# Cross attention of a Perceiver block: the norm and bias of the keys applied at the scores, the last key tiles of two batches shared, and the ternary weights' sums on another engine

## Chip, cores and metric

One NeuronCore of a Trainium2 chip runs the whole program. The metric is the device time of one execution in microseconds (us); lower is better. The program is written in Bass with the Tile layer, whose scheduler puts the instructions of each engine in a fixed order when the program is built. Engines are called TensorE (PE), VectorE (DVE), ScalarE (ACT), GpSimd (POOL) and SyncE (SP, which here issues every DMA).

## What is computed

A Perceiver block: 8 batches of 64 tokens with 512 features (`x`) attend to themselves and to a context of 1601 rows per batch (`ctx`); a small sparse attention and a ternary two-layer network follow. The change is in the attention to the context and in the preparation of the network's weights:

```
kx, vx = split(einsum(cond, w_kv_x))          # cond: 8 x 1601 x 512
kx = LN(kx) * kxln_w + kxln_b                 # over each head's 128 features, 8 key heads
p  = softmax(qx . kx / sqrt(128))             # 2 query heads for each key head
xout = p . vx
...
scale = mean(abs(w)); w = sign(w) * (abs(w) >= 0.7 * scale)    # both ffn weights
```

All matrix products are held to float32 accuracy: an operand is split into a high part in a rounded format (float32r) and the rest, and three products (high-high, high-rest, rest-high) are added in PSUM.

## The kernel before

**Units and tiles.** The context attention is cut into 16 units, one for each half of the key heads (4 heads, `HG`) and each batch: `Cross(b, half)`. The half is the outer loop. A unit's 1601 keys are 13 tiles: twelve of 128 keys and a last one of 65. The tiles form six chunks (`CHUNKS`, line 36): five of two tiles (256 keys), and a last one of three (128 + 128 + 65 = 321 keys).

**One key tile.** `keys` (line 529) loads 128 columns of the transposed context (`cTr`), ScalarE makes the high part (`cThi`, 536), GpSimd the rest (`cTlo`, 537), and TensorE runs twelve matmuls with 512 moving columns (542), the context standing in the array and the key weights moving. The weights have had each head's mean taken off (`key_weights`), so the product needs no mean. ScalarE squares it (547) and copies it to `kn` (548); VectorE sums the squares per head (549); GpSimd adds epsilon (550) and raises to the power -1/2 (`rsqrt`, line 173, tile `rqk`); VectorE multiplies `kn` by that (552). `keys_t` (555) transposes `kn` on TensorE (219), and makes the two parts of the keys, with the norm's weight and bias: `kthi` on ScalarE (565), the rest on VectorE (`kf`, 567), and again ScalarE for the bias (`ktlo`, 568).

**Scores.** `scores` (570) multiplies the queries with a chunk's keys (587) into a PSUM bank of the pool `pm` (three banks, tag `m`, shared with the transposes of the probabilities `pt` and others); each bank holds two heads' scores, or one's in the last chunk. A custom VectorE operation (591) copies the scores to SBUF, adding zeros, and keeps the row's maximum. `maxima` (594) forms the maximum of a unit, `exps` (598) the exponentials on ScalarE (601). `probs_t` (604) transposes the probabilities and splits them (`phi`, `plo`, 623 and 624), `context` (636) loads the context rows again (`cr`) and splits them (`chi`, `clo`), and `weigh` (661) sums probability times context over the 13 tiles (676 to 678, accumulators `acc`).

**Order.** The main loop (line 1142) runs one key tile per step: keys of tile g, their transposition one step later, scores of a chunk two steps after its last key tile, probabilities and context 16 to 17 steps behind (`LAG`). Into each step generators put other work at a given pace: projections and self-attention (`bgA`), the last parts (`bgC`), and `ternary` (918, `bgB`), which reads both network weights in 32 pieces, sums their absolute values on VectorE (926), and then reads them again to make the ternary weights. The scheduler then orders all engines' instructions; SP's list of DMAs is one queue, and a DMA that waits for an engine holds up those behind it.

Of the kernel before, what the change touches and what calls it, by code (L numbers as in the profile page):

```python
# [11 lines left out]
F32 = mybir.dt.float32  # L12
# [9 lines left out]
P = 128  # L22
H = 512
NIC = 4
# [12 lines left out]
KTW = 324  # L37
NCH = len(CHUNKS)
CHUNK_OF = {tt: ci for ci, ch in enumerate(CHUNKS) for tt in ch}
LAG = 17  # L40
# [6 lines left out]
LATER = 142  # L47
TERNARY_PACE, TERNARY_AT = 0.4, 8
HELD = "held"

# [7 lines left out]
def tile_perceiver(ctx: ExitStack, tc: tile.TileContext, t: dict):  # L58
# [18 lines left out]
    def nm(s):  # L77
        uid[0] += 1
        return f"{s}_{uid[0]}"
# [62 lines left out]
    class Late:  # L142
# [11 lines left out]
        xrt = _main("qxhi", 1)  # L154
        pd = _main("kf", 2)
        ps = staticmethod(lambda tag="b": kxp())
# [334 lines left out]
    def key_weights(half):  # L491
        hi = mp.tile([P, NIC, 512], F32R, tag="wkhi", name=nm("wkhi"), bufs=1)
        lo = mp.tile([P, NIC, 512], F32R, tag="wklo", name=nm("wklo"), bufs=1)
        for ic in range(NIC):
            tag, bufs = ("kf", 2) if half == 0 and ic >= 2 else ("raw", 3)
            raw = load(mp.tile([P, 512], F32, tag=tag, name=nm("wkr"), bufs=bufs), t["wkv"][ic * P:(ic + 1) * P, half * 512:(half + 1) * 512])
            raw3 = v3(raw, HG)
            mu = sm("wkmu", HG)
            V.tensor_reduce(mu, raw3, AX.X, ALU.add)
            V.scalar_tensor_tensor(raw3, mu.unsqueeze(2).to_broadcast([P, HG, D]), -1.0 / D, raw3, ALU.mult, ALU.add)  # L500
            A.copy(hi[:, ic, :], raw)
            (V if half else GP).tensor_tensor(lo[:, ic, :], raw, hi[:, ic, :].bitcast(F32), ALU.subtract)
        return hi, lo

    paced = [None]
    pin = [None]

    class Cross:


        def __init__(self, b, half):
            self.b, self.half = b, half
            self.raw = None
            self.S = {}
            self.kt = {}
            self.kn = {}
            self.pp = {}
            self.cc = {}
            self.mx = sm("cmx", HG * NCH, bufs=2)
            self.su = sm("csu", HG * NCH, bufs=2)  # L520

# [7 lines left out]
        def keys(self, tt):  # L529

            t0, n = TT[tt]
            raw = mp.tile([P, NIC, P], F32, tag="raw", name=nm("cTr"), bufs=3)
            paced[0] = nc.sync.dma_start(raw[:, :, :n], t["ctxT"][self.b].rearrange("(c p) k -> p c k", p=P)[:, :, t0:t0 + n])
            chi = mp.tile([P, NIC, P], F32R, tag="cThi", name=nm("cThi"), bufs=2)
            clo = mp.tile([P, NIC, P], F32R, tag="cTlo", name=nm("cTlo"), bufs=2)
            A.copy(chi[:, :, :n], raw[:, :, :n])  # L536
            GP.tensor_tensor(clo[:, :, :n], raw[:, :, :n], chi[:, :, :n].bitcast(F32), ALU.subtract)  # L537
            ps = kxp()
            k = 0
            for st, mv in ((chi, self.wk[0]), (chi, self.wk[1]), (clo, self.wk[0])):  # L540
                for ic in range(NIC):
                    PE.matmul(ps[:n], lhsT=st[:, ic, :n], rhs=mv[:, ic, :], start=k == 0, stop=k == 11)  # L542
                    k += 1
            kn = mp.tile([P, 512], F32, tag="kn", name=nm("kn"), bufs=3)
            sq = mp.tile([P, 512], F32, tag="sq", name=nm("sq"), bufs=1)
            v = sm("kxv", HG)
            A.activation(sq[:n], ps[:n], AF.Square, scale=1.0 / math.sqrt(D))  # L547
            A.copy(kn[:n], ps[:n])
            V.tensor_reduce(v[:n], v3(sq[:n], HG), AX.X, ALU.add)  # L549
            GP.tensor_scalar(v[:n], v[:n], EPS, None, ALU.add)  # L550
            r = rsqrt(v[:n], n, HG, "rqk")
            pin[0] = V.tensor_tensor(v3(kn[:n], HG), v3(kn[:n], HG), r.unsqueeze(2).to_broadcast([n, HG, D]), ALU.mult)  # L552
            self.kn[tt] = kn

        def keys_t(self, tt):

            t0, n = TT[tt]
            ci = CHUNK_OF[tt]
            c0 = TT[CHUNKS[ci][0]][0]
            if ci not in self.kt:  # L560
                self.kt[ci] = [mp.tile([P, HG, KTW], F32R, tag="kt" + x, name=nm("kt" + x), bufs=2) for x in ("hi", "lo")]
            hi, lo = self.kt[ci]
            pt = transpose4(self.kn.pop(tt), n, kxp())
            o = slice(t0 - c0, t0 - c0 + n)
            A.activation(hi[:, :, o], v3(pt, HG)[:, :, :n], AF.Identity, bias=hb["kx"], scale=hw["kx"])  # L565
            kf = mp.tile([P, HG, P], F32, tag="kf", name=nm("kf"), bufs=2)
            V.scalar_tensor_tensor(kf[:, :, :n], v3(pt, HG)[:, :, :n], hw["kx"], hi[:, :, o].bitcast(F32), ALU.mult, ALU.subtract)  # L567
            A.activation(lo[:, :, o], kf[:, :, :n], AF.Identity, bias=hb["kx"])  # L568

        def scores(self, ci):  # L570
# [3 lines left out]
            N = cw + (cw & 1)  # L574
            if N > cw:
                GP.memset(hi[:, :, cw:N].bitcast(F32), 0.0)
                GP.memset(lo[:, :, cw:N].bitcast(F32), 0.0)
            sc = mp.tile([P, HG, KTW], F32, tag="S", name=nm("S"), bufs=7)
            self.S[ci] = sc
            per = 512 // N  # L580
            for g0 in range(0, HG, per):
# [7 lines left out]
                for i, g in enumerate(gs):  # L589
                    ps = bank[:, i * N:(i + 1) * N]  # L590
                    V.tensor_tensor_reduce(sc[:, g, :cw], ps[:, :cw], zeros.to_broadcast([P, cw]), 1.0, -3.0e38,  # L591
                                           ALU.add, ALU.max, self.mx[:, g * NCH + ci:g * NCH + ci + 1])

        def maxima(self):
            self.nmx = sm("cnm", HG)
            V.tensor_reduce(self.nmx, v3(self.mx, HG), AX.X, ALU.max, negate=True)  # L596

# [320 lines left out]
    def ternary(name, dst):  # L918
# [4 lines left out]
        for k in range(nr * ncb):  # L923
            r, cb = k // ncb, k % ncb
            raw = load(tern(), w[r * P:(r + 1) * P, cb * 512:(cb + 1) * 512])
            V.tensor_reduce(su[:, k:k + 1], raw, AX.X, ALU.add, apply_absolute_value=True)
            yield
# [17 lines left out]
    def ffn_rows(pairs, kind):  # L945
# [22 lines left out]
        return z, xs  # L968

    def gp_copy(dst, src):  # L970
        GP.tensor_scalar(dst, src, 1.0, 1.0, ALU.mult, ALU.mult)  # L971

# [156 lines left out]

    NT = len(TT)  # L1130
    work = [Cross(b, half) for half in range(2) for b in range(NB)]
# [10 lines left out]
    for g in range(NA + LAG + 3):  # L1142
# [25 lines left out]
        if g < NA:  # L1168
            work[nA].keys(kA)
        if g == 0:  # L1170
            bgA.pump(ALL)
        if g == 2:
            bgA.add(norms(rest), projection("qx", range(4), rest), projection("qx", range(4, 8), range(NJ)),
                    projection("q", range(8), range(NJ)), projection("k", range(4), range(NJ)), projection("v", range(4), range(NJ)))
            bgA.add(*[self_attn(j) for j in range(NJ)])
            bgA.add(attn_consts())
# [132 lines left out]
```

## Time and profile before

| | us |
|---|---|
| runs: median (lowest to highest of 3) | 2002.96 (2000.17 to 2003.44) |
| the profiled execution: its time / its span | 1998.47 / 1996.7 |
| TensorE idle, 0 to 100 us | 24.2 |
| TensorE idle, 100 to 1800 us | 25.0 |
| TensorE idle, 1800 to 1997 us | 16.3 |

The span is from the first to the last instruction that the profiler recorded; the execution's time is 1.8 us more. "Busy" for TensorE is the union of its matmuls' records, which overlap, so small gaps between them are not seen in it.

A row of a group gives line, engine, operation, the tiles written and read, the shape, how many, then the busy time and the mean duration of one, and the idle time of the engine before them with what ended it. Two of them:

```
L568 ACT ACTIVATE ktlo<-kf,cols 128x512 fp32r<-128x512 f32 (+1 forms) x208 | 147.4, 709 | 29.0 <-DVE kf L567 28.5
L552 DVE TENSOR_TENSOR kn<-kn,rqk 128x512 f32<-128x512 f32 (+1 forms) x208 | 144.7, 695 | 57.0 <-POOL rqk L173 55.5
```

A row of a timeline gives start and length in us, engine, line, operation, tiles, the size of the array used, the shape and the number of instructions merged.

### The profile page before, as it was taken

What the parts mean: (1) busy time and instruction counts of PE and PEld (TensorE: products, weight loads), DVE (VectorE), ACT (ScalarE), POOL (GpSimd) and SP (SyncE); (2) the same over time, 40 slices, a digit from 0 to 9 for tenths busy, and PEclk for the clock granted to TensorE, in tenths of its full rate; (3) what the DMA queues carried; (4) which work ended last, traced back from release to release, by engine and by line L of the source; (5) the groups of instructions that cost most, each with busy time, mean ns of one, the idle gap of its engine ahead of it and who ended that gap; (6) DMA issues with size and microseconds to landing.
All of it is one profiled execution on the core that took longest, in us unless ns stands there. A gap on an engine that the chain in (4) does not pass through costs nothing. (4 is left out here: it accounts for less than half of the span.)

```text
span 1996.7 us, 32526 instructions
## 1 busy us (share of the span) xinstructions
PE 1931.5 (97%) x10709; PEld 1594.1 (80%) x10709; DVE 1357.9 (68%) x3324; ACT 1345.9 (67%) x2932; POOL 682.7 (34%) x807
## 2 busy tenths in 40 slices
PE   6899999999999999999999999999999999999998
PEld 5688887888888888888888888888877777886776
DVE  6868678667778677766775765666577665665665
ACT  6777777677778667765765655665786676676554
POOL 5443434333334434323233323323333323320132
PEclk9999999999999999999999999999999999999989
DMA  6354445466455654556886667656744633564415
GB/s 195 112 151 148 148 146 153 132 193 213 152 150 172 194 179 140 173 180 224 282 268 192 214 225 264 203 185 214 258 133 154 212 110 97 165 205 139 149 56 172
DMA packets 296507, 352.05 MB, mean 176 GB/s; under 512 B 30337, under 2 KB 191233, under 8 KB 296337
## 3 DMA queue, kind: packets, MB, share of 16 engines
q1 hardware_dynamic: 296336, 349.97, 55.8%
q8 instruction: 84, 1.38, 0.3%
q14 instruction: 87, 0.70, 0.1%
HBM read 283.94 MB, written 65.68 MB: 175 GB/s over the span
## 5 line engine op out<-in xcount | busy, mean ns | idle before, releaser
L537 POOL TENSOR_TENSOR cTlo<-cTr,cThi 128x512 fp32r<-128x512 f32 (+1 forms) x208 | 271.1, 1303 | 840.7 <-PE kx L542 443.8
L677 PE MATMUL acc<-plo,chi 128*128 128x512 f32 x768 | 311.7, 406 | 1.0 <-DVE plo L624 1.0
L678 PE MATMUL acc<-phi,clo 128*128 128x512 f32 x768 | 303.4, 396 | 0.0
L549 DVE TENSOR_REDUCE kxv<-sq 128x4 f32<-128x512 f32 (+1 forms) x208 | 141.9, 682 | 228.0 <-ACT sq L547 227.7
L542 PE MATMUL kx<-wkhi,cThi 128*128 128x512 f32 (+1 forms) x832 | 244.3, 415 | 6.6 <-DVE cmx L591 2.5
L676 PE MATMUL acc<-phi,chi 128*128 128x512 f32 x768 | 237.8, 403 | 4.6 <-ACT chi L653 3.4
L565 ACT ACTIVATE kthi<-kx,cols 128x512 fp32r<-128x512 f32 (+1 forms) x208 | 159.5, 767 | 106.8 <-PE kx L219 105.1
L542 PE MATMUL kx<-wklo,cThi 128*128 128x512 f32 (+1 forms) x832 | 231.0, 398 | 0.0
L542 PE MATMUL kx<-wkhi,cTlo 128*128 128x512 f32 (+1 forms) x832 | 226.3, 393 | 0.0
L173 POOL TENSOR_TENSOR rqk<-kxv,mhalf 128x4 f32<-128x4 f32 (+1 forms) x208 | 219.9, 1057 | 16.6
L653 ACT CAST chi<-cr 128x512 fp32r<-128x512 f32 x192 | 118.9, 619 | 137.7 <-PE acc L677 126.2
L536 ACT CAST cThi<-cTr 128x512 fp32r<-128x512 f32 (+1 forms) x208 | 125.6, 605 | 120.0 <-PE kx L542 48.4
L601 ACT ACTIVATE S<-S,cnm 128x256 f32<-128x256 f32 (+1 forms) x384 | 196.8, 520 | 1.5 <-DVE cnm L596 1.5
L567 DVE SCALAR_TENSOR_TENSOR kf<-kx,cols,kthi 128x512 f32<-128x512 f32 (+1 forms) x208 | 151.1, 726 | 60.0 <-ACT kthi L565 58.8
L542 PEld LDWEIGHTS kx<-wklo,cThi 128*128 128x128 f32 (+1 forms) x832 | 156.2, 188 | 39.7
L542 PEld LDWEIGHTS kx<-wkhi,cTlo 128*128 128x128 f32 (+1 forms) x832 | 153.5, 185 | 39.3 <-issue 0.8
L552 DVE TENSOR_TENSOR kn<-kn,rqk 128x512 f32<-128x512 f32 (+1 forms) x208 | 144.7, 695 | 57.0 <-POOL rqk L173 55.5
L542 PEld LDWEIGHTS kx<-wkhi,cThi 128*128 128x128 f32 (+1 forms) x832 | 147.2, 189 | 40.8 <-DVE cmx L591 5.0
L591 DVE CUSTOM_DVE_ANT_0 S<-s,zeros 128x256 f32<-128x256 f32 (+1 forms) x384 | 149.7, 429 | 43.8 <-PE s L587 43.5
L568 ACT ACTIVATE ktlo<-kf,cols 128x512 fp32r<-128x512 f32 (+1 forms) x208 | 147.4, 709 | 29.0 <-DVE kf L567 28.5
L676 PEld LDWEIGHTS acc<-phi,chi 128*128 128x128 f32 x768 | 139.0, 189 | 34.9 <-ACT chi L653 4.6
L677 PEld LDWEIGHTS acc<-plo,chi 128*128 128x128 f32 x768 | 145.2, 189 | 25.7 <-DVE plo L624 1.5
(339 smaller groups left out, 3938.3 us busy)
## 6 DMA issues: line engine op xcount, KB each, us to landing
cTr<-in_ctxT SPq DMA_DIRECT2D x192, 256.0 KB
cr<-in_ctx SPq DMA_DIRECT2D x192, 256.0 KB
ws<-wpd SPq DMA_DIRECT2D x88, 512.0 KB
clod<-clo SPq DMA_DIRECT2D x96, 256.0 KB
clo<-clod SPq DMA_DIRECT2D x96, 256.0 KB
wv<-in_wkv SPq DMA_DIRECT2D x64, 256.0 KB
tern<-in_ffn_w SPq DMA_DIRECT2D x64, 256.0 KB
wpd<-ws SPq DMA_DIRECT2D x32, 512.0 KB
```

The source lines that it names most:

```text
L173: GP.tensor_tensor(y[:n], v, mhalf[:n, :k], ALU.pow)
L537: GP.tensor_tensor(clo[:, :, :n], raw[:, :, :n], chi[:, :, :n].bitcast(F32), ALU.subtract)
L542: PE.matmul(ps[:n], lhsT=st[:, ic, :n], rhs=mv[:, ic, :], start=k == 0, stop=k == 11)
L552: pin[0] = V.tensor_tensor(v3(kn[:n], HG), v3(kn[:n], HG), r.unsqueeze(2).to_broadcast([n, HG, D]), ALU.mult)
L565: A.activation(hi[:, :, o], v3(pt, HG)[:, :, :n], AF.Identity, bias=hb["kx"], scale=hw["kx"])
L567: V.scalar_tensor_tensor(kf[:, :, :n], v3(pt, HG)[:, :, :n], hw["kx"], hi[:, :, o].bitcast(F32), ALU.mult, ALU.subtract)
L568: A.activation(lo[:, :, o], kf[:, :, :n], AF.Identity, bias=hb["kx"])
L591: V.tensor_tensor_reduce(sc[:, g, :cw], ps[:, :cw], zeros.to_broadcast([P, cw]), 1.0, -3.0e38, ALU.add, ALU.max, self.mx[:, g * NCH + ci:g ...
L601: A.activation(self.S[ci][:, g, :cw], self.S[ci][:, g, :cw], AF.Exp, bias=self.nmx[:, g:g + 1], accum_out=self.su[:, g * NCH + ci:g * NCH ...
L676: PE.matmul(self.U[ic], lhsT=chi[:n, s], rhs=phi[:n], start=tt == 0, stop=False)
L677: PE.matmul(self.U[ic], lhsT=chi[:n, s], rhs=plo[:n], start=False, stop=False)
L678: PE.matmul(self.U[ic], lhsT=clo[:n, s], rhs=phi[:n], start=False, stop=False)
```

## The change

1. **Norm at the scores.** A key's factor r (one per key and head) is no longer multiplied into `kn`. The raw keys are transposed; `turned` makes both parts with the norm's weight alone. r is stored to DRAM tile by tile (`rd`), and when a chunk's last tile is stored, `spread` loads the chunk's values into all 128 partitions (`rb`, keys by heads, 324 x 4 floats, two buffers). The VectorE operation of the scores multiplies by `rb[:, :cw, g]` in place of adding zeros.
2. **Bias at the scores.** The norm's bias adds the same number to all of a row's scores, which a softmax does not see. It stands as one more column behind the last chunk's 321 keys (the place of a zero column before), its score is copied to `qb`, and `maxima` forms the maximum as qb - (max + qb).
3. **Paired last tiles.** From batch 2 of half 0 on, the last tile's first 64 keys of two batches share one tile of 128: the even batch computes it (tile `kn2`, factors `rt`), the odd one has no thirteenth key tile. The remaining key 1600 of all eight batches is computed once for each half by `odd_keys`, at steps 30 and 110; its transposed parts are copied behind the 64 keys.
4. **Absolute sums on ScalarE.** `ternary` forms them with an activation (absolute value, with a running sum) in place of VectorE's reduction.
5. The buffers `kf` give way to `rb`; the program is built with `dynamic_dma_scratch_size=1024`.

The core of the diff:

```diff
+NT = len(TT)
+ODD_AT = 30, 110
+UNPAIRED = 2
+RB = 2
...
+    def raw_keys(wk, chi, clo, n, held=False):
+
+        ps = kxp()
+        k = 0
+        for st, mv in ((chi, wk[0]), (chi, wk[1]), (clo, wk[0])):
+            for ic in range(NIC):
+                PE.matmul(ps[:n], lhsT=st[:, ic, :n], rhs=mv[:, ic, :], start=k == 0, stop=k == 11)
+                k += 1
+        kn = mp.tile([P, 512], F32, tag="kn2" if held else "kn", name=nm("kn"), bufs=1 if held else 3)
+        sq = mp.tile([P, 512], F32, tag="sq", name=nm("sq"), bufs=1)
+        v = sm("kxv", HG)
+        A.activation(sq[:n], ps[:n], AF.Square, scale=1.0 / math.sqrt(D))
+        A.copy(kn[:n], ps[:n])
+        pin[0] = V.tensor_reduce(v[:n], v3(sq[:n], HG), AX.X, ALU.add)
+        GP.tensor_scalar(v[:n], v[:n], EPS, None, ALU.add)
+        r = rsqrt(v[:n], n, HG, "rqk")
+        return kn, r
+
+    def turned(kn, n, parts, r0=0):
+
+        hi, lo = parts
+        pt = kxp()
+        for g in range(HG):
+            PE.transpose(pt[:, g * P:g * P + n], kn[:, g * P:(g + 1) * P], ident[r0:r0 + n, r0:r0 + n])
+        src = v3(pt, HG)[:, :, :n]
+        A.activation(hi, src, AF.Copy, scale=hw["kx"])
+        V.scalar_tensor_tensor(lo, src, hw["kx"], hi.bitcast(F32), ALU.mult, ALU.subtract)
+
+    def odd_keys(half):
+
+        raw = load(mp.tile([P, 512], F32, tag="raw", name=nm("oc"), bufs=3)[:NB], t["ctx"][:, SC - 1, :])
+        pt = kxp()
+        for ic in range(NIC):
+            PE.transpose(pt[:, ic * NB:(ic + 1) * NB], raw[:, ic * P:(ic + 1) * P], ident[:NB, :NB])
...
+        kn, r = raw_keys(wk[half], chi, clo, NB)
+        oddr[half] = dtile([NB, HG], F32, f"oddr{half}")
+        nc.sync.dma_start(oddr[half], r)
...
+        turned(kn[:NB], NB, [x[:, :, :, 0] for x in oddk[half]])
...
         def keys(self, tt):
...
+            pair = tt == NT - 1 and self.paired
+            if pair and self.b % 2:
+                return
...
-            pin[0] = V.tensor_tensor(v3(kn[:n], HG), v3(kn[:n], HG), r.unsqueeze(2).to_broadcast([n, HG, D]), ALU.mult)
+            kn, r = raw_keys(self.wk, chi, clo, n, pair)
             self.kn[tt] = kn
+            if pair:
+                nxt = work[self.half * NB + self.b + 1]
+                nxt.kn[tt] = kn
+                self.rt = nxt.rt = dram.tile([P, HG], F32, tag="rt", name=nm("rt"), bufs=2)
+                nc.sync.dma_start(self.rt, r)
+                return
...
+            nc.sync.dma_start(self.rd[ci][o:o + n], r)
+
+        def spread(self, ci):
+            cw = sum(TT[tt][1] for tt in CHUNKS[ci])
+            rb = self.rb[ci] = mp.tile([P, KTW, HG], F32, tag="rb", name=nm("rb"), bufs=RB)
+            parts = [(0, self.rd.pop(ci)[:cw])]
+            if ci == NCH - 1 and self.paired:
+                o = cw - S - 1
+                parts = [(0, parts[0][1][:o]), (o, self.rt[self.b % 2 * S:(self.b % 2 + 1) * S]), (cw - 1, oddr[self.half][self.b:self.b + 1])]
+            for o, src in parts:
+                w = src.shape[0]
+                load(rb[:, o:o + w].rearrange("p t g -> p (t g)"), src.rearrange("t g -> (t g)").partition_broadcast(P))
...
-            A.activation(hi[:, :, o], v3(pt, HG)[:, :, :n], AF.Identity, bias=hb["kx"], scale=hw["kx"])
-            kf = mp.tile([P, HG, P], F32, tag="kf", name=nm("kf"), bufs=2)
-            V.scalar_tensor_tensor(kf[:, :, :n], v3(pt, HG)[:, :, :n], hw["kx"], hi[:, :, o].bitcast(F32), ALU.mult, ALU.subtract)
-            A.activation(lo[:, :, o], kf[:, :, :n], AF.Identity, bias=hb["kx"])
...
-                    V.tensor_tensor_reduce(sc[:, g, :cw], ps[:, :cw], zeros.to_broadcast([P, cw]), 1.0, -3.0e38,
-                                           ALU.add, ALU.max, self.mx[:, g * NCH + ci:g * NCH + ci + 1])
+                    V.tensor_tensor_reduce(sc[:, g, :cw], ps[:, :cw], rb[:, :cw, g], 1.0, -3.0e38,
+                                           ALU.mult, ALU.max, self.mx[:, g * NCH + ci:g * NCH + ci + 1])
+                    if N > cw:
+                        V.tensor_copy(self.qb[:, g:g + 1], ps[:, cw:N])
 
         def maxima(self):
+
+            top = sm("ctop", HG)
+            V.tensor_reduce(top, v3(self.mx, HG), AX.X, ALU.max)
+            V.tensor_tensor(top, top, self.qb, ALU.add)
             self.nmx = sm("cnm", HG)
-            V.tensor_reduce(self.nmx, v3(self.mx, HG), AX.X, ALU.max, negate=True)
+            V.tensor_tensor(self.nmx, self.qb, top, ALU.subtract)
...
-            V.tensor_reduce(su[:, k:k + 1], raw, AX.X, ALU.add, apply_absolute_value=True)
+            A.activation(raw, raw, AF.Abs, accum_out=su[:, k:k + 1])
...
         if g < NA:
             work[nA].keys(kA)
+            if kA == CHUNKS[CHUNK_OF[kA]][-1]:
+                work[nA].spread(CHUNK_OF[kA])
...
+        if g in ODD_AT:
+            odd_keys(work[nA].half)
```

## The prediction

> **What bounds the kernel now.** I read the engines' shares of the page first, then the same by stretch.
>
> ```profile
> PE 1931.5 (97%) x10709; PEld 1594.1 (80%) x10709; DVE 1357.9 (68%) x3324; ACT 1345.9 (67%) x2932; POOL 682.7 (34%) x807
> ...
> q1 hardware_dynamic: 296336, 349.97, 55.8%
> ```
> ```profile
> 0.00:100.00 100.00, 75.82 (x382) 61.57 (x383) 76.31 (x215) 71.43 (x149) 51.82 (x67) 0.94 0.51 154
> 100.00:1800.00 1700.00, 1674.99 (x9332) 1398.89 (x9332) 1161.25 (x2827) 1167.78 (x2580) 587.08 (x692) 0.99 0.58 183
> 1800.00:1997.00 197.00, 180.73 (x998) 133.59 (x994) 120.37 (x283) 106.64 (x206) 43.78 (x49) 0.94 0.43 130
> ```
>
> The columns of the second are length, then busy time of PE, PEld, DVE, ACT and POOL, then clock, DMA share and GB/s. In the 1700 us of key work TensorE lacks only 25 us; VectorE and ScalarE stand at 68%. So a microsecond counts only if it is taken from TensorE's list, or from a wait of TensorE. The chain that ended last covers only the last 25 us, the two-layer network at the end, which the change does not touch. A matmul's record overlaps the next one's, so its 390 ns is not its price. The price is from one start to the next; the timeline of one last key tile gives it:
>
> ```profile
> 1109.59 1.17 PE L542 MATMUL kx<-wkhi,cThi 128*65 128x512 f32 x4
> 1110.59 1.09 PE L542 MATMUL kx<-wklo,cThi 128*65 128x512 f32 x4
> 1111.52 1.09 PE L542 MATMUL kx<-wkhi,cTlo 128*65 128x512 f32 x4
> 1112.55 1.16 PE L485 MATMUL po<-fb,ld 64*128 64x128 f32 x8
> ```
>
> Twelve matmuls from 1109.59 to 1112.55: 2.96 us for 65 keys. A full tile next to it (1118.71, 1119.72, 1120.64) steps at the same 0.92 to 1.01 us per four. The 512 moving columns set the price, not the keys.
>
> **Pairing of the last tiles.** In the built order of the changed kernel 201 key tiles stand where 208 did, seven fewer (three in half 0, four in half 1), and two tiles of eight keys come in (odd_keys). Removed: 7 x 2.96 = 20.7 us (by steps of 0.92: 19.3). Added: 2 x 2.96 = 5.9 us (5.5), and 16 transposes of 8 rows, by the 128-wide rows of 0.35 to 0.44 us per four 0.1 us each, 1.6 us. All this lies on TensorE: -13.2 us (-12.2 to -13.5). TensorE's other matmuls are the same in number and shape. The odd unit's missing tile also spares ScalarE and GpSimd five tiles net, 9 and 13 us there, hidden. The kept tile kn2 has one buffer, but its next writer comes 25 tiles later: no wait.
>
> **Norm moved to the scores, off the path.** Rows by line (busy us, mean ns), then TensorE's waits:
>
> ```profile
> L591 DVE CUSTOM_DVE_ANT_0 S<-s,zeros 128x256 f32<-128x256 f32 x320 | 119.7, 418 | 28.5 <-PE s L587 28.3
> ...
> L897 DVE TENSOR_REDUCE ao<-pr 128x64 f32<-128x384 f32 x3 | 2.5, 832 | 0.0
> ...
> L926 DVE TENSOR_REDUCE tsumffn_w<-tern 128x1 f32<-128x512 f32 x32 | 21.7, 679 | 0.0
> ```
> ```profile
> PE pt L613 <- DVE cmx L591: 3.9, 5, 1.4
> ...
> PE kx L219 <- DVE kn L552: 3.0, 2, 1.9
> ...
> PE kx L542 <- DVE cmx L591: 2.5, 6, 0.6
> ```
>
> VectorE loses the 208 products of L552 (144.7 us) and the 32 sums of L926 (21.7). It gains 64 copies of one column from PSUM (164 ns by the copy of L817: 10 us) and two 128x4 operations for each of 16 maxima (169 ns by L596: 5 us). ScalarE loses the 208 passes of L568 (147.4 us) and gains 32 absolute sums: 630 ns as L803, plus 197 ns for the accumulator as in L601, 26 us. No table load is added in the built order.
>
> The score operation now reads rb with a step of four floats. The row: a step of two floats (L885) costs nothing, 357 ns for 192 elements; a step of 64 floats (L897) costs 832 ns for 384, where a plain product of 384 (L882) takes 552, so 0.73 ns more for each. No row has a step of four. The Trainium skill ("SBUF — State Buffer", under "Door 1: The DMA port swizzle") says that SBUF is read in lines of 16 bytes and that a stream which takes one element from each line pays; four floats is exactly there. By the row of L885 the operation stays at 418 ns and the sum on VectorE is -151 us. By the rule with L897's size it takes 418 + 256 x 0.73 = 605 ns, 384 of them add 75 us, and the sum is -76 us. I take the rule. Either way VectorE ends below 68%. What this can touch is the PSUM bank: a bank holds two groups, so it is freed 0.4 us later. TensorE waited for such a bank eleven times (6.4 us); eleven times 0.4 is 4 us, the lower queue of VectorE gives some back, so +2 us (0 to +8).
>
> What goes from TensorE's waits: L219 no longer waits for the product, -3.0 us (both waits fall in the first 60 us); and with VectorE relieved by 76 us and ScalarE by some 125, part of the other 20 us of TensorE's waits on them, -2 us (0 to -8). If the new maxima chain were bare, 16 x 1 us would be lost; but TensorE waited only 2.8 us for the exponentials that hang on it, so I count it in the +2.
>
> **The new wait: r goes through DRAM.** Each tile's rqk is written out (207 small stores and 2 of eight rows), and a load of 512 KB spreads a chunk over the partitions (96, of which 14 have two small loads beside them), all on SP: 329 more DMAs than the 1368 in the built order. The score operation waits for it, and on VectorE everything stands behind that: the key sums L549, plo L624, the splits. Time needed, from the store and load of sim:
>
> ```profile
> 1488.23 2.30 SPq L830 DMA_DIRECT2D simd<-fa  x4
> 1491.78 0.50 SPq L130 DMA_DIRECT2D sim<-simd  x1
> ```
>
> The last of the four stores starts at 1490.03, and the load that waits for it goes out at 1491.78: 1.75 us (2.7 in another pass, at 1808). GpSimd reads sim at 1493.86, 2.1 us on. The spread moves 0.52 MB; at 350 MB in 55.8% of 1997 us the engines move 314 GB/s when busy, so 1.7 us more. Issue, store and load: 0.5 + 1.75 to 2.7 + 3.8 = 6 to 7 us. Time there is:
>
> ```profile
> 1115.90 1.09 POOL L173 TENSOR_TENSOR rqk<-kxv,mhalf 65x4 f32<-65x4 f32 x1
> ```
> ```profile
> 1129.32 0.49 DVE L591 CUSTOM_DVE_ANT_0 S<-s,zeros 128x321 f32<-128x321 f32 x1
> ```
>
> Here 12.3 us; over the 96 chunks the median is 16.0, the tenth lowest 12.3, the least 8.4. In the changed order, at the old steps, 17 us of matmuls (old: 16.3) lie between a chunk's last key matmul and its first score matmul, of which rqk takes 3.4; the first chunks have 9 to 12 us. So mid-kernel the load has 6 us in hand and costs nothing; in the first 100 us four chunks come 0.5 us late or so: +2 us (0 to +8). If that cover went, 96 chunks would pay.
>
> SP's queue: a store waits for GpSimd's rqk, and a spread for the store's landing, up to 2 us in the 33 chunks where they stand next to each other. Behind them stand the loads of keys (cTr) and of context (cr) and the stores of clo. SP waited up to 7.6 us in one place already. But cThi was ready 13.3 us (median) before the matmul that reads it, and chi 11.4 us, so a few microseconds there are covered: 0. DMA share: 52 MB more, 8 points by bytes and up to 5 by packets: 64 to 69%, hidden. The smaller scratch for dynamic DMA touches no queue that the profile shows: 0.
>
> **Sum.** -13.2 - 3.0 - 2 + 2 + 2 = -14.2 us. The profiled execution took 1998.47 us (span 1996.7 and 1.8 around it), so 1984.3. The median of the runs, 2002.96, lies 4.5 us higher: 1989 us.
>
> **Rivals.** *The spread comes late* (slower). Place: the score operation's wait for rb. If the way through DRAM and SP's queue takes 14 to 15 us instead of 6 to 7, more than the 13 us between rqk and the score matmuls, VectorE stands some 2 us in each of 96 chunks; TensorE has plo in hand by 3.45 us (median), 1.04 (tenth lowest), so about 0.5 us of each reaches it: +48 - 13 = +35, 2038 us. For it: SP's waits of 5 to 7 us, pieces of 16 bytes, one queue for all. Against: the 6 us in hand. It decides from about 13 us on. Chance 0.2. *Given back in small waits*: banks held longer (+8), start (+8), nothing gained on other waits: about 1999 to 2006, within 0.2% of before, which is about what a measurement of this kernel can tell from no change. Chance 0.08. *The relief counts for more*: TensorE's waits of the middle shrink by 8 to 10 us: 1979 us. Chance 0.08. That the change does not remove the matmuls is excluded by the built order.
>
> **Numbers.** The likeliest, 1989 us (own range 1982 to 1997), has 0.64. Faster by over 0.2%: 0.64 + 0.08 = 0.72; same 0.08; slower 0.20. The range from 1977 to 2012 takes in all but the far part of the late spread (0.14) and a little below.
>
> **What would show it.** Right: 201 full key tiles; TensorE's busy time down by about 13 us and still 97%; no wait of VectorE for rb past the first 100 us; the score row near 605 ns (418 would refute the rule here); VectorE near 1280, ScalarE near 1220 us; DMA share 64 to 69%. Wrong: a row in which S waits for rb with some 100 us, TensorE waiting for plo or for a bank, cThi waiting for cTr; or TensorE's share falling to 95%.

## The result, and the profile after

| | before | after |
|---|---|---|
| median of 4 runs each, us | 2003.16 | 2095.69 (2089.53 to 2101.72) |
| ratio, 95% interval | | 1.0465 (1.0432 to 1.0498) |
| profiled execution: time / span, us | 1998.47 / 1996.7 | 2089.53 / 2087.8 |
| clock granted to TensorE, mean share of the full one | 0.987 | 0.977 |

The change makes the kernel 92.5 us slower, where 1989 us had been forecast. From the profile's page of after, its engines and the hardware DMA queue:

```profile
PE 1959.4 (94%) x10665; PEld 1600.2 (77%) x10665; DVE 1297.7 (62%) x3182; ACT 1223.5 (59%) x2803; POOL 679.1 (33%) x766
...
q1 hardware_dynamic: 343068, 402.86, 64.3%
```

VectorE and ScalarE lost what had been forecast (1280 and 1220 us forecast, 1298 and 1224 found), and the DMA share lies at the lower end of the forecast 64 to 69%. But TensorE is busy 28 us longer instead of 13 us shorter, and its share has fallen to 94%. The stretches of after (length, then busy time of PE, PEld, DVE, ACT and POOL, clock, DMA share, GB/s):

```profile
0.00:100.00 100.00, 69.58 (x333) 57.40 (x334) 64.03 (x179) 55.26 (x119) 47.72 (x63) 0.88 0.56 165
100.00:1800.00 1700.00, 1621.55 (x8848) 1335.49 (x8847) 1059.27 (x2593) 1009.37 (x2358) 566.40 (x629) 0.98 0.67 202
1800.00:2088.00 288.00, 268.29 (x1487) 207.34 (x1486) 174.44 (x411) 158.84 (x327) 64.97 (x75) 0.97 0.52 159
```

In the 1700 us of key work TensorE now lacks 78 us where it lacked 25, and ends them 484 matmul records behind. The matmuls themselves are not slower where nothing disturbs them. One tile in the timeline of after:

```profile
1171.59 1.17 PE L527 MATMUL kx<-wkhi,cThi 128*128 128x512 f32 x4
1172.60 1.10 PE L527 MATMUL kx<-wklo,cThi 128*128 128x512 f32 x4
1173.54 1.08 PE L527 MATMUL kx<-wkhi,cTlo 128*128 128x512 f32 x4
1174.54 0.46 PE L544 MATMUL kx<-ident,kn 64*128 64x64 f32 x4
1178.07 1.22 PE L435 MATMUL pp<-ws,cats 128*128 128x512 f32 x2 [3.06 <-DMA ws<-wpd]
1179.09 1.48 PE L771 MATMUL acc<-phi,chi 128*128 128x512 f32 x3
```

Twelve matmuls from 1171.59 to 1174.54 take 2.95 us, as before. Then TensorE stands 3.06 us for a load of weights, and after the pause two matmuls take 1.02 us from start to start, twice their pace. The groups by shape, the score operation and the split of the loaded keys:

```profile
L680 DVE CUSTOM_DVE_ANT_0 S<-s,rb 128x256 f32<-128x256 f32 x320 | 179.3, 605 | 26.3 <-PE s L676 25.2 <-DMA cr<-in_ctx 0.8
L680 DVE CUSTOM_DVE_ANT_0 S<-s,rb 128x321 f32<-128x321 f32 x64 | 46.1, 721 | 15.3 <-PE s L676 10.7 <-DMA rb<-rd 2.7 <-DMA rb<-rt 1.8
L611 ACT CAST cThi<-cTr 128x512 fp32r<-128x512 f32 x199 | 123.7, 621 | 266.8 <-DMA cTr<-in_ctxT 168.7 <-PE kx L527 45.5 <-issue 34.4
```

The score operation takes 605 ns, the forecast number, and waits for `rb` 4.5 us in all (2.7 + 1.8). So r itself comes in time but for these; it is the other loads that are late. ScalarE waits 168.7 us for `cTr`. In the waits of before the same line was

```profile
ACT cThi L536 <- DMA cTr<-in_ctxT: 16.0, 16, 3.0
```

(us in all, times, longest) and in the waits of after, of ScalarE and TensorE:

```profile
ACT cThi L611 <- DMA cTr<-in_ctxT: 168.7, 64, 6.9
...
PE pp L435 <- DMA ws<-wpd: 16.4, 12, 3.1
...
PE s L676 <- DVE cmx L680: 8.1, 4, 3.7
PE pt L708 <- DVE cqb L683: 6.5, 5, 1.9
...
PE pt L708 <- DVE cmx L680: 3.9, 5, 1.8
```

What SP's queue waits for in after:

```profile
SPq L134 <- DMA rd<-rqk: 147.2, 78, 4.8
SPq L626 <- POOL rqk L177: 146.7, 127, 9.0
```

78 spreads stand 1.9 us each for a store to land, 127 stores 1.2 us each for GpSimd. One place in the timeline, SP and ScalarE:

```profile
1167.01 0.38 SPq L626 DMA_DIRECT2D rd<-rqk  x1
1167.48 0.38 SPq L134 DMA_DIRECT2D clo<-clod  x1
1170.12 0.32 SPq L134 DMA_DIRECT2D rb<-rd  x1
1170.49 0.43 SPq L608 DMA_DIRECT2D cTr<-in_ctxT  x1
1171.02 0.92 SPq L134 DMA_DIRECT2D ws<-wpd  x2
...
1176.85 0.62 ACT L611 CAST cThi<-cTr 128x512 fp32r<-128x512 f32 x1 [4.22 <-DMA cTr<-in_ctxT]
```

The spread goes out 3.1 us after the store; `cTr` and `ws` go out right behind it. ScalarE stands 4.22 us for `cTr`, and TensorE its 3.06 us for `ws` (above). This picture suggested the first theory: SP's in-order queue, held by the two new waits, delays the loads behind them. It is the theory that the experiments had to test.

### The profile page after: what moved, and what is told of

Its sections match the earlier page's. It is cut to its first block, busy times and chain, and to the rows that moved or that the text cites. A ratio compares the mean times of both kernels' runs of the same rounds, so it can differ in the third digit from the quotient of the medians.

```text
span 2087.8 us, 32963 instructions
## 1 busy us (share of the span) xinstructions
PE 1959.4 (94%) x10665; PEld 1600.2 (77%) x10665; DVE 1297.7 (62%) x3182; ACT 1223.5 (59%) x2803; POOL 679.1 (33%) x766
## 4 chain that ended last, share of the span: by engine, by line
PE 61%; DMA 20%; DVE 7%; ACT 5%; issue 3%; POOL 2%; SPq 1%; POOLq 0%; ACTq 0%; DVEq 0%
PE kx L527 19%; PE acc L771 6%; DMA cTr<-in_ctxT 6%; PE acc L772 6%; PE acc L773 5%; PE s L676 4%; PE pj L344 3%; PE pt L708 3%; PE kx L544 3%; DMA ws<-wpd 2%; PE xo L792 2%; DMA wpd<-ws 2%; PE pp L435 2%; DVE S L680 2%; PE p L900 1%
## 5 line engine op out<-in xcount | busy, mean ns | idle before, releaser
L612 POOL TENSOR_TENSOR cTlo<-cTr,cThi 128x512 fp32r<-128x512 f32 (+1 forms) x201 | 260.9, 1298 | 784.5 <-ACT cThi L611 396.8
L611 ACT CAST cThi<-cTr 128x512 fp32r<-128x512 f32 (+1 forms) x201 | 124.5, 619 | 268.3 <-DMA cTr<-in_ctxT 168.7
L680 DVE CUSTOM_DVE_ANT_0 S<-s,rb 128x256 f32<-128x256 f32 (+1 forms) x384 | 225.4, 625 | 41.6 <-PE s L676 36.0
L527 PE MATMUL kx<-wkhi,cThi 128*128 128x512 f32 x812 | 238.9, 415 | 12.5 <-ACT kn L533 3.3
L527 PE MATMUL kx<-wklo,cThi 128*128 128x512 f32 x812 | 230.8, 405 | 0.0
L527 PE MATMUL kx<-wkhi,cTlo 128*128 128x512 f32 x812 | 227.7, 399 | 0.0
L547 DVE SCALAR_TENSOR_TENSOR ktlo<-kx,cols,kthi 128x512 fp32r<-128x512 f32 (+2 forms) x208 | 150.7, 725 | 99.8 <-ACT kthi L546 98.6
L546 ACT ACTIVATE kthi<-kx,cols 128x512 fp32r<-128x512 f32 (+2 forms) x208 | 140.5, 676 | 79.8 <-PE kx L544 79.0
L527 PEld LDWEIGHTS kx<-wklo,cThi 128*128 128x128 f32 x812 | 155.8, 192 | 39.6 <-issue 1.6
L527 PEld LDWEIGHTS kx<-wkhi,cTlo 128*128 128x128 f32 x812 | 153.7, 190 | 39.8 <-issue 2.4
L527 PEld LDWEIGHTS kx<-wkhi,cThi 128*128 128x128 f32 x812 | 146.3, 192 | 48.4 <-DVE cmx L680 5.4
L773 PEld LDWEIGHTS acc<-phi,clo 128*128 128x128 f32 x768 | 145.5, 190 | 25.3 <-issue 0.8
```

Source lines behind the costliest of these rows:

```text
L546: A.activation(hi, src, AF.Copy, scale=hw["kx"])
L547: V.scalar_tensor_tensor(lo, src, hw["kx"], hi.bitcast(F32), ALU.mult, ALU.subtract)
L680: V.tensor_tensor_reduce(sc[:, g, :cw], ps[:, :cw], rb[:, :cw, g], 1.0, -3.0e38, ALU.mult, ALU.max, self.mx[:, g * NCH + ci:g * NCH + ci + 1])
L773: PE.matmul(self.U[ic], lhsT=clo[:n, s], rhs=phi[:n], start=False, stop=False)
```

## The experiments

"Over before" is the median of the run less that of before among the same job's runs (before lay between 1997.9 and 2000.8 us in the five jobs).

| run | us | over before | ratio, 95% interval |
|---|---|---|---|
| e1_norm_back | 2015.28 | +15.4 | 1.0089 (1.0062 to 1.0115) |
| e2_spread_only | 2041.63 | +41.8 | 1.0219 (1.0184 to 1.0255) |
| e3_trip_only | 2065.72 | +65.8 | 1.0336 (1.0306 to 1.0366) |
| e4_const_rb | 2023.37 | +23.5 | 1.0121 (1.0094 to 1.0147) |
| e5_sums_on_vector | 2017.92 | +17.2 | 1.0089 (1.0068 to 1.0111) |
| e6_no_bias_column | 2011.02 | +10.3 | 1.0060 (1.0039 to 1.0081) |
| e7_unpaired | 2015.35 | +14.6 | 1.0076 (1.0048 to 1.0104) |
| e8_before_abs | 2013.30 | +12.6 | 1.0064 (1.0043 to 1.0086) |
| e9_order_ternary | 2015.69 | +17.8 | 1.0082 (1.0061 to 1.0102) |
| e10_order_pace | 2000.27 | +2.3 | 1.0007 (0.9997 to 1.0018) |
| e11_gpsimd_queue | 2078.33 | +80.4 | 1.0388 (1.0358 to 1.0419) |
| e12_const_rb_step1 | 2008.89 | +11.0 | 1.0049 (1.0033 to 1.0065) |
| e13_stale_spread | 2086.18 | +85.5 | 1.0414 (1.0377 to 1.0451) |
| e14_stale_all | 2059.59 | +59.0 | 1.0294 (1.0271 to 1.0318) |
| e15_stores_only | 2051.14 | +50.5 | 1.0259 (1.0231 to 1.0287) |
| e16_pair_only | 2003.80 | +3.2 | 1.0009 (0.9995 to 1.0022) |
| e17_gp_stores | 2124.93 | +124.2 | 1.0609 (1.0568 to 1.0650) |
| e18_old_stores | 2080.37 | +79.6 | 1.0374 (1.0333 to 1.0415) |

### Which part of the change costs

**e1_norm_back** takes the norm back to VectorE, and with it all stores and spreads away:

```diff
+        pin[0] = V.tensor_tensor(v3(kn[:n], HG), v3(kn[:n], HG), r.unsqueeze(2).to_broadcast([n, HG, D]), ALU.mult)
...
-            nc.sync.dma_start(self.rd[ci][o:o + n], r)
...
-                    V.tensor_tensor_reduce(sc[:, g, :cw], ps[:, :cw], rb[:, :cw, g], 1.0, -3.0e38,
+                    V.tensor_tensor_reduce(sc[:, g, :cw], ps[:, :cw], zeros.to_broadcast([P, cw]), 1.0, -3.0e38,
```

> The changed kernel with the norm's factor multiplied into kn on VectorE again (no stores of r, no spread, scores copied with zeros); the bias column, the paired last tiles and the absolute sums on ScalarE stay. If the way of r through DRAM or the slower score operation costs the 93 us, this runs at 1985 to 1995 us, some 10 to 15 under the kernel before. If the pairing, the bias column, the sums on ScalarE or the new order of the program cost them, it stays above 2060 us.

**e2_spread_only** keeps the spreads, but reads them from rows of an input that is always there, and stores nothing:

```diff
-                self.rd[ci] = dram.tile([KTW, HG], F32, tag="rd", name=nm("rd"), bufs=3)
-            o = t0 - TT[CHUNKS[ci][0]][0]
-            nc.sync.dma_start(self.rd[ci][o:o + n], r)
+                self.rd[ci] = t["wkv"][self.b, :KTW * HG].rearrange("(t g) -> t g", g=HG)
```

> The changed kernel with the spread of each chunk loaded from rows of an input, and no stores of r: the same 52 MB of spread traffic, but nothing on SP waits for r or for a store's landing. The scores are scaled by other numbers than r. Theory of SP's queue (loads stand behind the store-and-spread trip): about 2010 us. Theory of traffic (the spreads hold the DMA engines and make the key loads land late): 2080 us or more, cThi still waiting for cTr with over 100 us. If both share it: near 2050.

**e3_trip_only** keeps the stores, and in place of the spread of 512 KB loads 2 KB of what was stored; the scores take a constant tile:

```diff
-                load(rb[:, o:o + w].rearrange("p t g -> p (t g)"), src.rearrange("t g -> (t g)").partition_broadcast(P))
+                load(rb[:min(w, P)], src[:min(w, P)])
...
-            rb = self.rb.pop(ci)
+            rb = rbc
```

> The changed kernel with the stores of r kept and each spread replaced by a load of the same stored values of 2 KB, on the same place in SP's queue and with the same wait for the store's landing; the score operation reads a constant tile of rb's layout. The scores are scaled by a constant in place of r. Theory of SP's queue: 2080 us. Theory of traffic: 2010 to 2020 us, cThi's wait for cTr back below 40 us.

**e4_const_rb** has the constant tile and neither stores nor loads of r.

> The changed kernel with neither stores nor spreads; the score operation reads a constant tile of rb's layout (step of four floats, 605 ns). The scores are scaled by a constant in place of r. If the trip or the traffic is the cause: 1990 to 2000 us. If the slower score operation, which frees its PSUM bank later, is the cause: 2060 us or more. TensorE's waits for banks freed by the score operation stay near 25 us in either case if they come from its length, and fall below 10 if they come from late keys.

e1, e3 and e4 fell between the two times that their texts give, e2 near the one for a shared cause. Counted from e4 (+23.5), the spread's traffic alone adds 18.3 us (e2), stores with a small load 42.3 (e3), and the two together, as in the changed kernel, 69.0 (92.5 - 23.5). So most of the loss belongs to the way through DRAM. For the stores this is not the new order alone: compared place by place in the traces, e15 below (stores and no load, 27.0 us over e4) has another instruction than e4 at 216 of ScalarE's 2803 places and e3 at 439, but e2 at 1110, so that the 18.3 of the spreads could be order (e9, below, measures a change of order alone). What is left without it, 15.4 us in e1, was still not the forecast gain of 13 us.

**e12_const_rb_step1** asks what the step of four floats costs. It is e4 with the same order of instructions; only the layout of the constant tile differs:

```diff
-    rbc = ctile([P, KTW, HG], F32, "rbc")
+    rbc = ctile([P, HG, KTW], F32, "rbc")
...
-                    V.tensor_tensor_reduce(sc[:, g, :cw], ps[:, :cw], rb[:, :cw, g], 1.0, -3.0e38,
+                    V.tensor_tensor_reduce(sc[:, g, :cw], ps[:, :cw], rb[:, g, :cw], 1.0, -3.0e38,
```

> As e4_const_rb (no stores, no spread, a constant tile in place of rb; the scores are multiplied by 0.05 instead of r), but the constant tile is laid out so that the score operation reads it with a step of one float instead of four; the order of the instructions is that of e4. If the 8 us between e4 and e1 are the score operation's length (605 against 418 ns): 418 ns again and about 2015. If they are the order: 2023 as e4, though the operation is short. A row that stays near 605 ns would say that not the step but the second SBUF operand costs.

The line's durations (ns, least/median/most, both shapes together), first in e4, then in e12:

```profile
L661 DVE CUSTOM_DVE_ANT_0 S<-s,rbc x384: 547/606/758, 51.8 to 1820.6; 128x256 f32<-128x256 f32 x160, 128x321 f32<-128x321 f32 x32
```
```profile
L661 DVE CUSTOM_DVE_ANT_0 S<-s,rbc x384: 372/420/495, 53.7 to 1806.2; 128x256 f32<-128x256 f32 x160, 128x321 f32<-128x321 f32 x32
```

The two traces have the same instructions in the same order on every engine. So the step is the cause of the length, and it costs 12.5 us of time (23.5 - 11.0; some 6 either way by the two intervals), not the 2 us of the sum.

### The smaller parts, and the order

The first three are e1 with one more part undone. **e5_sums_on_vector** forms the absolute sums on VectorE again (`V.tensor_reduce(..., apply_absolute_value=True)` for the activation):

> As e1_norm_back (2015 us), but the absolute sums are formed on VectorE again. e1 lies 15 us above before where its 60 fewer matmuls promised 13 below, so some 28 us are to be found. Theory that ScalarE, which now stands in order before a late weight load (31 us in 17 waits in e1, no such wait on VectorE before), passes this on: 1995 to 2003 us. Theory that the longer maxima chain or the pairing costs it: 2013 to 2018 us.

**e6_no_bias_column** leaves the bias out of the maximum (a constant of each row, which the softmax does not see), without the copies `qb` and with one operation for the maximum:

> As e1_norm_back, but the bias column's score is not copied and the maximum is formed by one operation, as before the change (the bias, which cancels in the softmax, drops out). In e1 it takes 3.0 us on average from a unit's last score operation to the finished maximum, 0.8 before. If these three chained operations cost the 28 us: 1995 us or less. If the sums on ScalarE or the pairing do: 2012 us or more.

**e7_unpaired** sets `self.paired = False` and `ODD_AT = ()`:

> As e1_norm_back, but no last tile is shared and there are no odd keys: 208 key tiles, 60 matmuls more. If the pairing is worth its matmuls: 2028 us. If the uneven steps of the pairing (an odd unit has twelve key tiles) cost the 28 us: 2000 us or less.

**e8_before_abs** is the kernel before with the absolute sums on ScalarE alone:

> The kernel before with only the absolute sums moved to ScalarE. Theory that ScalarE's wait for the weight loads matters: 2010 to 2018 us. Otherwise 1998 to 2004 us, no difference from before.

Undoing one part of e1 does not bring the time back: all five kernels (e1 among them) lie 10 to 17 us over before, even e8, which changes only 32 instructions. e8 took the time that its text gives for the theory of ScalarE's waits, but e5, which undoes the same sums in e1, gains nothing. What all five have in common is that the scheduler draws the order anew. Two further kernels were to test that: before, with one constant changed and the same instructions.

```diff
-TERNARY_PACE, TERNARY_AT = 0.4, 8
+TERNARY_PACE, TERNARY_AT = 0.4, 12
```

> The kernel before with one constant changed: the quantizing of the ternary weights joins its background list at tile 12 instead of tile 8. No instruction is added or removed; only the order in which the engines' instructions stand changes. If the 10 to 15 us that every variant of the change loses, even the small ones, come from the order alone (the order of before being a favourable draw): 2007 to 2016. If they come from what the variants compute: 2001, within 4 us of before.

```diff
-LATER = 142
+LATER = 130
```

> The kernel before with the tile from which the background work runs at its slower pace moved from 142 to 130: again the same instructions, and an order that differs in few places (some 400 of TensorE's instructions stand elsewhere). Order theory: a smaller loss than with the ternary shift or none, 2001 to 2010. Theory of the work: 2001.

The middle stretch of e9, to be laid beside that of before (1674.99 us of TensorE, 9332 matmuls):

```profile
100.00:1800.00 1700.00, 1662.63 (x9249) 1387.09 (x9250) 1165.35 (x2806) 1157.20 (x2556) 589.37 (x690) 0.99 0.57 181
```

With the same work, e9 loses 17.8 us. e10 (+2.3, interval 0.9997 to 1.0018) is no test of the order: by line, operation, tile and shape its trace has every engine's instructions in the order of before. So a new order alone can cost what e1 and its variants cost, by one sample of it; differences of this size between two of them say nothing sure about the part that was undone.

**e16_pair_only** is e1 with the edits of e5 and e6 together. Of the change it keeps the pairing, and also ScalarE's lack of the second pass over the keys (L568 of before, 147.4 us), since the bias is not taken in the copies, as its text says, but dropped, as in e6.

> The pairing of the last tiles alone: the kernel before with it, the norm multiplied in on VectorE, the bias taken in the copies, and the absolute sums on VectorE. By the removed matmuls alone it should take 1987 to 1990. If the order's draw hides it as it did in the other variants (2011 to 2018): 2005 to 2016. Below 1998 it would beat both kernels.

It takes as long as before (1.0009, interval 0.9995 to 1.0022). It is the fastest of the variants that hold a part of the change, and beats nothing. That it is 12 us faster than e1 would also fit a cost of some 10 us for the sums on ScalarE or for the bias column; between that and the order the runs do not decide.

### Why the way through DRAM costs

**e11_gpsimd_queue** issues stores and spreads from GpSimd (`nc.gpsimd.dma_start` for `nc.sync.dma_start`):

> The changed kernel with the stores of r and the spreads of r issued by GpSimd instead of SyncE; all else on SyncE as it was. If the in-order queue of SyncE is what costs (stores that wait for GpSimd and spreads that wait for the stores' landing hold the loads of keys, weights and context behind them): ScalarE's wait for cTr falls from 169 us to below 60, and the time to about 2040 (the spread's traffic alone gave 2042). If the transfers themselves are what costs (small packets on the shared DMA engines): cTr stays above 120 us, time 2080 to 2095. If GpSimd's own queue becomes the place of the standing (it forms cTlo and rqk): TensorE waits for cTlo, 2080 to 2120.

SP hardly waits for `rd` or `rqk` any more (`rqk` 1.9 us in all). ScalarE still waits 157.7 us for `cTr`, and the gain over the changed kernel is only 12 us (92.5 - 80.4). GpSimd now stands for the landing:

```profile
POOL rb L637 <- DMA rd<-rqk: 146.0, 42, 7.6
```

GpSimd forms `cTlo`, which frees the buffer of a later `cTr`; the wait had changed its engine, so this was no clean test. The next three give the same DMAs old data. **e13_stale_spread** reads the chunk two before and gives `rb` three buffers; **e14_stale_all** also stores the tile two before:

```diff
+            prev.append(own)
+            old = prev[max(0, len(prev) - 3)]
...
+                full.append(r)
+                r = full[-3] if len(full) > 2 else full[0]
```

> The changed kernel in which the spread of a chunk reads the stored norms of the chunk two before (long landed), and rb has three buffers instead of two; so the scores are multiplied by the wrong norms. Stores, spreads and bytes are as in the changed kernel; only SyncE's wait for the landing of a store that has just gone out is taken away. If that wait is what holds the loads behind it: SyncE's wait for rd goes from 147 us to near 0, and the time falls by 20 to 35 us, to 2060 to 2075. If it is the waiting of the stores for GpSimd's rqk, or the traffic itself: 2085 to 2097.

> As e13_stale_spread, and each store writes the norms of the tile two before (already formed), so that neither stores nor spreads wait for anything fresh: the traffic and SyncE's list of the changed kernel without both waits (the norms that reach the scores are again wrong ones). If the in-order queue is the larger part: near the spread's traffic alone (2042), 2038 to 2052. If the small packets and the 329 more issues are the larger part: 2075 to 2095.

e13 did not do what it should. The scheduler moved the spreads forward until they again met fresh stores (the waits of SP in e13):

```profile
SPq L628 <- POOL rqk L177: 160.1, 128, 9.2
...
SPq L134 <- DMA rd<-rqk: 102.3, 53, 4.9
```

In e14 the wait for the landing is nearly gone (4.7 us), that for `rqk` is 114 us with 3.9 at most, and the time falls by 33.5 us (92.5 - 59.0). That spoke for the queue, though some of it can be order. **e15_stores_only** is e3 without the small load:

> As e4_const_rb (a constant tile in place of rb), but each tile's norms are still stored, and nothing reads them: 209 stores of 16-byte pieces, each waiting for GpSimd's rqk on SyncE, no load, no wait for a landing. e4 took 2023, and stores together with a small load 2066. If the landing wait is the cost: 2023 to 2032. If the stores (their wait for rqk, their small packets) are: 2050 to 2066.

The stores alone cost 27.0 us over e4, more than the landing wait and the small load add to them (15.3). The last two runs ask whether a store costs because it stands in SP's list until GpSimd has formed r. **e17_gp_stores** issues the real stores from GpSimd, the spreads from SP; **e18_old_stores** is e15 with the r of the tile four before, each store held behind its own tile's load:

```diff
+                r = full[-5] if len(full) > 4 else full[0]
...
+            with tc.issue_after(paced[0].ins):
+                nc.sync.dma_start(self.rd[ci][o:o + n], r)
```

> The changed kernel with the 209 stores of r issued by GpSimd, which has formed r itself and so does not wait; the spreads stay on SyncE. Stores alone cost 28 us over e4 (e15). If that is their place in SyncE's list, where each waits for GpSimd: 2062 to 2075 here, and SyncE's wait for rqk is gone. If it is the stores themselves (packets, descriptors): about 2090.

> As e15_stores_only, but each store writes the norms of the tile four before and is held behind the load of its own tile in SyncE's list, so that what it writes was formed about one tile (9 us) before its turn; as many stores, bytes and packets, nothing reads them. e15 took 2051, e4 (no stores) 2023. If the stores' wait for GpSimd holds the queue: 2023 to 2032, and SyncE's wait for rqk falls from 168 us to below 30. If the 16-byte packets or the issues cost: 2043 to 2055.

Neither bears it out: both are slower than either time that their texts give. In e18 the stores wait 5.1 us in all for `rqk` (168.1 in e15); SP's first lines are waits of the kind that before has too:

```profile
SPq L611 <- POOL kxv L536: 194.9, 68, 11.5
SPq L134 <- PE acc L782: 123.7, 68, 7.8
```

(In before the first is 223.0 us.) Yet it is 29 us slower than e15, and e17 is 32 us slower than the changed kernel. In e17 the wait for `rqk` is gone as well, and that for the landing has grown, as has GpSimd's work, so it too is no clean test:

```profile
SPq L134 <- DMA rd<-rqk: 220.6, 81, 5.8
```

So SP's waits alone do not set the price; in all SP waits 1431 us in before and 1346 in after. What goes with the time, though not strictly, is how long ScalarE stands for transfers of any kind. Its rows of the waits view added up, and the middle time (median) from the issue of `cTr` to `cThi`, for those tiles where ScalarE stood for it:

| run | us | ScalarE's waits for transfers, us | issue of `cTr` to `cThi`, us |
|---|---|---|---|
| before | 1999 | 50 | 4.4 |
| e1 | 2015 | 137 | 4.6 |
| e12 | 2009 | 161 | 4.4 |
| e4 | 2023 | 150 | 4.2 |
| e15, stores | 2051 | 186 | 4.3 |
| e2, spreads | 2042 | 202 | 4.7 |
| e3, stores and small load | 2066 | 215 | 4.7 |
| e18, old stores | 2080 | 220 | 4.9 |
| e14, old data in both | 2060 | 249 | 5.2 |
| e13, old data in spreads | 2086 | 256 | 5.0 |
| e11, GpSimd's queue | 2078 | 267 | 4.9 |
| after | 2096 | 269 | 5.1 |
| e17, stores by GpSimd | 2125 | 287 | 5.1 |

Part of ScalarE's standing is idle time that it had gained (50 to some 140 us cost 15 us at most, order included). From e4 on, more standing mostly goes with a longer run. e14 is the clear exception: with 249 us it runs faster than e3 with 215 and e18 with 220. Behind `cThi` on ScalarE stand the squares and copies of the keys, `chi` and `phi`, and TensorE waits for those. But ScalarE is only one of the ways to TensorE. TensorE's rows of the waits view, added up by what it waited for:

| run | for VectorE, us | for ScalarE, us | for a load, us |
|---|---|---|---|
| before | 28.5 | 21.6 | 6.6 |
| e12 | 34.6 | 30.6 | 9.0 |
| e4 | 45.4 | 31.0 | 9.2 |
| after | 54.9 | 43.2 | 21.4 |

From e4 to after each of the three grows by about as much: 9.5, 12.2 and 12.2 us. Late loads reach TensorE through ScalarE, as loads of its own (`ws`, `wv`), and by way of VectorE.

## Why the prediction was wrong

**What bounds the kernel.** The reading held: a microsecond counts only at TensorE, and a matmul's price is its step. It was TensorE's waits that went wrong.

**Pairing, -13.2.** The matmuls did go. If each matmul is charged the time to the next one's start, and steps more than 0.3 us over the median of their kind are set apart as pauses, the rest lies between 1912 and 1918 us in the five kernels without the pairing (before and e7 to e10), and between 1903 and 1911 in e1, e5, e6 and e16: by the averages 9 us fewer, so the term was about right, if somewhat large. It did not show as time: e7 and e1 are equal (+14.6 and +15.4), and e16 lies at +3.2. What the pairing gave was lost among other waits of TensorE; in e16 the pauses sum to 85 us, in before to 66.

**Score operation, 605 ns; price +2.** The rule of the Trainium skill ("SBUF — State Buffer", "Door 1: The DMA port swizzle"), that each access to a new line of 16 bytes pays, held at a step of four floats, against the row of L885. The page gives no size; the 0.73 ns came from L897, another operation with a step of 64, and that it fitted to the nanosecond is in part luck. The price was mis-sized: 12.5 us. Between e12 and e4 TensorE's waits for VectorE grow by 10.8 us, and 7.5 of these are for the score operation and the copy behind it (5.1 us in 8 waits, 12.6 in 20). The sum had lengthened the waits that were there; new ones came.

**The new wait, +2.** The score operation's wait for `rb` is 4.5 us, as the sum had it, and the rival *The spread comes late* fell in its place, though it was the only case on the right side (2038 us).

**"SP's queue ... covered: 0" and "DMA share ... hidden".** This is the step that failed. The way through DRAM costs 69 us over e4, where the sum had 0. The working had looked at the lead of `cThi` before its own matmul (13.3 us, median), and that lead is still there (13.5). But a late load stops ScalarE (168.7 us for `cTr`, 16.0 in before), and what stands behind `cThi` on ScalarE need not have such a lead; and TensorE's own waits for loads, which the step left out, grew from 6.6 to 21.4 us. Whether the queue or the traffic makes the loads late is not settled (see Open). The prediction asked for this about VectorE and `rb` and did not ask it about ScalarE and `cTr`. "cThi waiting for cTr" and "TensorE's share falling to 95%", which it had named as signs of being wrong, both came. Two counts of that part were off, without weight in the sum: there are 203 stores, not 209 (the 329 more DMAs are right), and the longest wait of SP in before is 17.9 us, not 7.6.

**Order, taken as given.** A term was missing: the built order was read for its counts alone. e9 shows that a new order can cost 17.8 us with the same work. Of the 92.5 us, 69 are the way through DRAM (with whatever the new order adds or takes), 12.5 the step of four, and 11 are left in e12, within what e9 lost by its order.

**Open.** Within the 69 us, stores (27 us by e15, in nearly the order of e4) count; the spreads' 18 (e2) are no more than an order can cost; and together they cost more than the sum of the two. Whether a store costs by its place in a list, by its 128 pieces of 16 bytes on the engines that carry the loads, or by the order that the scheduler draws around it, is not settled: e14 (less by 33.5 us) speaks for the waits in SP's list, e17 and e18 against them, and each also has another order. No run took ScalarE's standing away and left the transfers, so its share of the 69 us is argued from the waits, not shown.

## What to carry to other kernels

When a new transfer is put on a queue that carries an engine's loads, ask not only how early the loaded tile is needed, but what stands behind the instruction that first reads it: an in-order engine that stands 4 us for a load holds up for 4 us everything after it that has no time in hand. Before a gain of less than one per cent is read into a kernel whose order a scheduler draws, run the kernel before in another order: here that alone was worth 18 us. A layout that makes VectorE read every fourth float can cost time even where VectorE is far from full: here 12.5 us with VectorE busy for 64% of the span (e4).

## What was not expected of the hardware

**A pause of TensorE costs again after it.** In the timeline of before:

```profile
897.42 0.79 PE L676 MATMUL acc<-phi,chi 128*128 128x512 f32 x1 [2.82 <-ACT chi L653]
898.01 0.63 PE L677 MATMUL acc<-plo,chi 128*128 128x512 f32 x1
898.43 0.63 PE L676 MATMUL acc<-phi,chi 128*128 128x512 f32 x1
```

After 2.82 us of standing, the matmuls step 0.42 to 0.43 us (from the second step on) where 0.23 is usual. The stretches around it (length, busy times, then clock, DMA share and GB/s) show the granted clock at half:

```profile
894.00:897.00 3.00, 0.59 (x6) 0.46 (x5) 1.66 (x3) 0.29 (x2) 1.26 (x2) 0.87 0.84 262
897.00:899.00 2.00, 1.58 (x4) 1.29 (x5) 1.60 (x3) 1.72 (x4) 0.66 (x1) 0.50 0.77 277
903.00:906.00 3.00, 3.00 (x16) 2.61 (x16) 1.55 (x5) 1.17 (x2) 1.29 (x1) 0.99 0.43 148
```

In the runs with more pauses the mean granted clock is lower: 0.987 in before, 0.977 in after, 0.970 in e17. In after, all steps outside the pauses sum to 1932 us against 1907 in e12, which has the same matmuls: 25 us beside the 57 us by which the pauses themselves grew (142 against 84). The mean clocks (0.977 of 2088 us, 0.986 of 2005) put the time lost to the lower clock at 48 and 28 us, an estimate that leaves some 20 of the 25 to the clock.

**GpSimd's issue of a DMA is not free.** The stores of e17 by their line (ns, least/median/most):

```profile
L626 POOL DMA_DIRECT2D rd<-rqk x194: 598/636/807, 23.2 to 1903.3; - x194
```

SP's issue of a spread in the same run takes 327 ns (median). GpSimd's busy time rose from 679 to 801 us.
